# The feed-forward rows of the last two pairs turned by TensorE in halves, in a gated cross-attention block

## The chip, the cores and the metric

The kernel runs on one core of one Trainium2 chip. The metric is the device time of one execution in microseconds (us); of several executions the median counts. The engines are called by their names in the profile: PE (TensorE, with PEld for its weight loads), DVE (VectorE), ACT (ScalarE), POOL (GpSimd) and SP (SyncE, which here only issues DMAs).

## What is computed

A block of Flamingo's kind: 16 batches of 224 tokens of 512 channels attend to up to 750 context rows each, and then pass a feed-forward layer whose two products are quantised ("bitlinear": the rows to 8-bit whole numbers, the weights to -1, 0, 1). The reference, cut to what matters:

```python
def bitlinear(x, w, b):
    xq = act_quant(rmsnorm(x))      # row / rms, then round(row * 127 / max|row|)
    wq = weight_quant(w)            # -1, 0, 1, times a scale
    return einsum('bsd,fd->bsf', xq, wq) + b

def ffn(x):                         # 512 -> 2048 -> 512
    h = bitlinear(x, w1, b1)
    h = gelu(h, approximate=False)
    return bitlinear(h, w2, b2)

x = x + tanh(g_xattn) * attention(layernorm(x), ctx, mask, W_q, W_k, W_v, W_o, b_o)
x = x + tanh(g_ffn) * ffn(layernorm(x))
```

## The kernel before

The masked context rows are left out before the attention, and the batches are sorted by how many rows remain; the token rows follow in that order. The feed-forward doesn't care for batches: it works on the 3584 token rows as 28 tiles of 128 rows, two tiles to a pair, 14 pairs (0 to 13). While batch `s` is in its attention, the feed-forward pieces of earlier pairs are merged between the attention's pieces by their estimated costs. After the last batch there are still pair 12's up product and pair 13's whole way to do. This tail is written out by hand at the end of `compact_path`, and nothing else runs beside it. A scheduler fixes each engine's order when the kernel is built, by the order of the calls and by its own cost estimates, so the program that runs has one fixed list of instructions per engine, and semaphores between them.

The stages of one tile (`k` is 0 or 1, `i` the pair), with their lines:

- `project` and `normalise`: the attention's output product (PE L1214), the residual `y` (DVE L1217), the normalised and rounded row `xq`, which a DMA transpose on SP turns into `xqT` (L1262). On POOL, small steps give the row's factor `c1`, and `b2` is added to `y` (L1272).
- `up(i, k, g)`, g = 0, 1: eight fp8 products of 512 columns into a PSUM tile `hp` (PE L1284), then `h = hp * c1 + b1` for 1024 columns on DVE (L1292). `hp` has two buffers. `h`, 2048 columns in fp32, has two buffers, so that pair 13's tile 0 takes the memory of pair 12's tile 0.
- `gelu(i, (k,))`: Gelu on ACT in place (L1304), the row's largest magnitude on DVE (L1307), its inverse (L1225, L1226), the product rounded into int16 (`hq`, L1310), a cast of that to bf16 (L1311), and a DMA transpose on SP, `hqT<-hq` (L1313). Then ACT squares `h` in place and sums the squares (L1315), and POOL makes of the sum, in five small steps (L1317, L794, L1233 to L1235), the factor `c2`.
- `down(i, k)`: sixteen fp8 products of 512 columns with `hqT` as weights into the PSUM tile `fp` (PE L1329), `y = fp * c2 + y` on DVE (L1333), and the row write to memory, an indirect DMA that POOL issues (L1335).

`fp`, like the turned tiles of other stages, is taken from a PSUM pool of four buffers (`gen`). The tail interleaves these stages so:

```python
for k in range(2):
    project(i, k)
    normalise(i, (k,))                                  # i = 13
downs = down_pieces(i - 1) + down_pieces(i)
for _, piece in up_pieces(i - 1):                       # pair 12
    piece()
for _, piece in weave(up_pieces(i), downs[:2]) + downs[2:]:
    piece()
```

The memory that the change takes for itself: `pT` holds the turned attention weights of one batch (12 x 224 floats per partition) and `xoT` the attention's output of the last four batches (4 x 896 floats); both are read for the last time before the tail's up products.

Of the kernel before, what the change touches and what calls it, by code (L numbers as in the profile page):

```python
# [16 lines left out]
EPS = 1e-5  # L17
# [716 lines left out]
def compact_path(ctx, tc, sh, x, context, out, late_loads, stages):  # L734
# [3 lines left out]
    nc = tc.nc  # L738
    P = 128
    B, S, D = x.shape  # L740
    _, J, C = context.shape
    FF = sh.FF
# [4 lines left out]
    ND = D // P  # L747
    NC = C // P
    NF = FF // P
    NP = HEADS // 2  # L750
    NB = 512
# [445 lines left out]
    pairs = {}  # L1197
    late = {}
# [24 lines left out]
    def quantiser(amax, part, least, name):  # L1223
        k = small(f"k_{name}")
        nc.vector.tensor_scalar(k[:, part], amax[:, part], least, 1.0 / 127.0, ALU.max, ALU.mult)  # L1225
        nc.vector.reciprocal(k[:, part], k[:, part])  # L1226
        load["v"] += 300
        return k

    def unquantiser(amax, r, part, isw, name):  # L1230

        c = small(f"c_{name}")
        nc.gpsimd.tensor_tensor(c[:, part], amax[:, part], r[:, part], ALU.mult)  # L1233
        nc.gpsimd.tensor_scalar(c[:, part], c[:, part], 1e-5, None, ALU.max)
        nc.gpsimd.tensor_scalar(c[:, part], c[:, part], isw, None, ALU.mult)  # L1235
        return c
# [38 lines left out]
    def up(i, k, g):  # L1275
        f = pairs[i]
        if g == 0:
            f["h", k] = pa.tile([P, FF], F32, tag="h", name=f"h_{i}_{k}", bufs=2)
        h = f["h", k]
        ph = wide([P, 2, NB], F32, f"hp_{i}_{k}_{g}")  # L1280
        for n in range(2):
            at = (2 * g + n) * NB
            for d in range(ND):
                nc.tensor.matmul(  # L1284
                    ph[:, n, :],
                    lhsT=f["xqT"][:, k * ND + d, :],
                    rhs=w1T[:, d, at : at + NB],
                    start=(d == 0),
                    stop=(d == ND - 1),
                )  # L1290
        cols = slice(2 * g * NB, 2 * (g + 1) * NB)
        nc.vector.scalar_tensor_tensor(  # L1292
            h[:, cols], ph.rearrange("t i n -> t (i n)"), f["c1", k], sh.b1[:, cols], ALU.mult, ALU.add
        )
        load["v"] += 1280

    def gelu(i, ks=(0, 1)):
        f = pairs[i]
        name = f"{i}_{ks[0]}"
        part = slice(ks[0], ks[-1] + 1)  # L1300
        ss = small(f"ss_{name}")
        amax = small(f"a2_{name}")
        for k in ks:
            nc.scalar.activation(f["h", k], f["h", k], AF.Gelu)  # L1304
        for k in ks:
            h = f["h", k]
            nc.vector.tensor_reduce(amax[:, k : k + 1], h, AX.X, ALU.max, apply_absolute_value=True)  # L1307
            scale = quantiser(amax, slice(k, k + 1), 1e-5 * EPS**0.5, f"2_{i}_{k}")
            hq = late["rows"].tile([P, FF], BF16, tag="hq", name=f"hq_{i}_{k}", bufs=3)
            nc.vector.tensor_scalar(hq.bitcast(I16), h, scale[:, k : k + 1], None, ALU.mult)  # L1310
            nc.vector.tensor_copy(hq, hq.bitcast(I16))  # L1311
            f["hqT", k] = hqT = late["rows"].tile([P, NF, P], BF16, tag="hqT", name=f"hqT_{i}_{k}", bufs=2)
            nc.sync.dma_start_transpose(out=hqT, in_=hq)  # L1313
        for k in ks:
            nc.scalar.activation(f["h", k], f["h", k], AF.Square, accum_out=ss[:, k : k + 1])  # L1315
# [6 lines left out]
        load["v"] += len(ks) * (2282 + 1280 + 690)  # L1322
        load["s"] += len(ks) * 2 * 1910 + 2600

    def down(i, k):
        f = pairs[i]
        po = gen([P, D], F32, f"fp_{i}_{k}")
        for n in range(NF):
            nc.tensor.matmul(  # L1329
                po, lhsT=f["hqT", k][:, n, :], rhs=w2T[:, n, :], start=(n == 0), stop=(n == NF - 1)  # L1330
            )
        y = f["y"][:, k, :]
        nc.vector.scalar_tensor_tensor(y, po, f["c2", k], y, ALU.mult, ALU.add)  # L1333
        load["v"] += 700
        nc.gpsimd.indirect_dma_start(  # L1335
            out=out_rows,
            out_offset=bass.IndirectOffsetOnAxis(ap=token(2 * i + k), axis=0),
            in_=y,
            in_offset=None,
            bounds_check=B * S - 1,  # L1340
            oob_is_err=False,
        )

    NPAIR = NTOK // 2

    def up_pieces(i):
        p = []
        for k in range(2):
            p += [(1.8, lambda g=g, k=k: up(i, k, g)) for g in range(2)]
            p.append((0.0, lambda k=k: gelu(i, (k,))))  # L1350
        return p

    def down_pieces(i):
        return [(3.5, lambda k=k: down(i, k)) for k in range(2)]

    def project_pieces(i):
        p = [(1.8, lambda k=k: project(i, k)) for k in range(2)]
# [134 lines left out]
    _, normed_first = norm_first(0)  # L1492
# [5 lines left out]
    pa = ctx.enter_context(tc.tile_pool(name="pa", bufs=1))  # L1498
# [39 lines left out]
    for s in range(B):  # L1538
# [35 lines left out]
    i = NPAIR - 1  # L1574
    residual(i)
    for k in range(2):
        project(i, k)
        normalise(i, (k,))
    downs = down_pieces(i - 1) + down_pieces(i)
    for _, piece in up_pieces(i - 1):  # L1580
        piece()
    for _, piece in weave(up_pieces(i), downs[:2]) + downs[2:]:
        piece()

# [31 lines left out]
```

## Time and profile before

| | |
|---|---|
| median of 3 runs | 751.12 us |
| lowest, highest | 750.07, 753.04 us |
| the profiled execution | 751.76 us |
| span in the profile | 750.0 us |
| mean granted PE clock | 0.976 |
| last row write issued by POOL | 737.75 us from the start of the span |

Busy time over the span, from the page: PE 681.3 us (91%), PEld 434.5 (58%), DVE 499.0 (67%), ACT 408.0 (54%), POOL 394.1 (53%). The tail from 697 on is 53 us, 7% of the span, and has its own limits, which the shares of the whole don't tell.

How the views are read. A row of the timeline has the start, the length, the engine, the line of the kernel, the operation, what it writes and reads with the shapes, and the count of instructions merged; in brackets stands how long the engine had been idle and what it waited for. A row of the windows has for each engine the busy time and the count of instructions in that stretch, then the granted clock of PE as a share of full speed, the DMA engines' busy share and the GB/s moved. A row by form has the busy time in all, the mean ns of one instruction, and the idle time before. The matmuls' ends are modelled; the times of POOL are rough.

### The profile page before, as it was taken

The numbers are of one execution on the slowest core, as the hardware profiler recorded it, in microseconds if no ns is written. First come the engines' busy times: TensorE is split into PE (matmuls) and PEld (weight loads), VectorE is DVE, ScalarE is ACT, GpSimd is POOL, SyncE is SP. The second block draws the span as 40 slices with busy tenths as digits, with TensorE's granted clock in tenths as the row PEclk, the third lists the DMA queues.
The fourth block names the chain that finished last, engine by engine and source line by source line (L and its number), as shares of the span: only waits on it lengthen the run. The fifth ranks groups of instructions, "written<-read, shape, count | busy, mean of one in ns | idle before, by whom it ended". The sixth has DMA issues, their size and how long they took to land.

```text
span 750.0 us, 11362 instructions
## 1 busy us (share of the span) xinstructions
PE 681.3 (91%) x3900; PEld 434.5 (58%) x3900; DVE 499.0 (67%) x1284; ACT 408.0 (54%) x963; POOL 394.1 (53%) x541
## 2 busy tenths in 40 slices
PE   4998899999999999997999999999999999988652
PEld 3776677675656565665655665666666566443211
DVE  5586846876684684755758675588584939586860
ACT  2549645383673846635757368365565656460530
POOL 5583676463654644547366564565654453636141
PEclk9989999999999999999999999999999999999887
DMA  7794031022222312222142413123132222214250
GB/s 240 270 285 140 25 90 31 15 73 57 76 48 62 95 43 74 50 66 73 28 99 68 85 54 68 43 72 79 55 62 65 56 71 57 71 29 78 41 108 31
DMA packets 87218, 58.77 MB, mean 78 GB/s; under 512 B 75488, under 2 KB 75632, under 8 KB 87024
## 3 DMA queue, kind: packets, MB, share of 16 engines
q1 hardware_dynamic: 79024, 32.00, 18.6%
q0 software_dynamic: 8128, 25.96, 11.0%
q8 instruction: 33, 0.54, 0.3%
q14 instruction: 33, 0.27, 0.1%
HBM read 32.26 MB, written 7.34 MB: 53 GB/s over the span
## 4 chain that ended last, share of the span: by engine, by line
PE 55%; issue 13%; DVE 12%; POOL 11%; DMA 4%; ACT 3%; POOLq 0%; DVEq 0%; ACTq 0%; SPq 0%
PE qp L1035 9%; PE op L1214 9%; PE fp L1329 7%; PE hp L1284 6%; PE kp L916 5%; PE sim L1074 4%; PE vp L931 4%; POOL p L1108 2%; PE ptp L1128 2%; DVE a L1307 2%; PE av L1151 2%; DVE h L1292 2%; DMA hqT<-hq 2%; DVE hq L1310 1%; POOL y L1272 1%
## 5 line engine op out<-in xcount | busy, mean ns | idle before, releaser
L1108 POOL TENSOR_TENSOR p<-p,rec 112x768 f32<-112x768 f32 (+1 forms) x64 | 84.3, 1318 | 73.6 <-DVE rec L1107 28.5
L1329 PE MATMUL fp<-w2T,hqT 128*128 128x512 fp8e4 x448 | 104.5, 388 | 13.6 <-DMA hqT<-hq 13.6
L1284 PE MATMUL hp<-w1T,xqT 128*128 128x512 fp8e4 x448 | 107.1, 384 | 8.8 <-DVE h L1292 6.1
L1098 ACT ACTIVATE p<-p,nm 112x192 f32<-112x192 f32 (+1 forms) x256 | 106.5, 420 | 8.0 <-DVE nm L1088 7.8
L1035 PE MATMUL qp<-xnT,wq_sb 128*128 128x224 f32 x512 | 105.8, 361 | 0.6 <-ACT xnT L780 0.6
L1214 PE MATMUL op<-wo_sb,xoT 128*128 128x512 f32 x224 | 103.7, 599 | 0.0
L1035 PEld LDWEIGHTS qp<-xnT,wq_sb 128*128 128x128 f32 x512 | 97.5, 194 | 6.6 <-issue 3.3
L1292 DVE SCALAR_TENSOR_TENSOR h<-hp,c,b_bc 128x1024 f32<-128x1024 f32 x56 | 71.6, 1279 | 40.1 <-PE hp L1284 37.6
L1329 PEld LDWEIGHTS <-hqT 128*128 128x128 bf16 x448 | 43.3, 99 | 71.1 <-DMA hqT<-hq 16.7
L1088 DVE CUSTOM_DVE_ANT_0 p<-sim,mask 112x128 f32<-112x128 f32 (+1 forms) x224 | 57.9, 313 | 34.4 <-PE sim L1074 33.9
L1307 DVE TENSOR_REDUCE a<-h 128x1 f32<-128x2048 f32 x28 | 63.9, 2281 | 22.4 <-ACT h L1304 22.3
L1284 PEld LDWEIGHTS <-xqT 128*128 128x128 bf16 x448 | 43.2, 98 | 57.7 <-issue 15.4
L1333 DVE SCALAR_TENSOR_TENSOR y<-fp,c,y 128x512 f32<-128x512 f32 x28 | 20.9, 745 | 76.2 <-PE fp L1329 72.9
L1335 POOL DMA_INDIRECT out_dram<-y,token x28 | 30.9, 1104 | 75.9 <-DVE y L1333 70.4
L1315 ACT ACTIVATE h<-h 128x2048 f32<-128x2048 f32 x28 | 53.4, 1907 | 22.2 <-DVE hq L1310 14.8
L1304 ACT ACTIVATE h<-h 128x2048 f32<-128x2048 f32 x28 | 53.4, 1909 | 19.7 <-DVE k L1225 10.8
L916 PE MATMUL kp<-ctxT,wk_sb 128*128 128x192 f32 (+1 forms) x384 | 63.3, 314 | 0.0
L1214 PEld LDWEIGHTS op<-wo_sb,xoT 128*128 128x128 f32 x224 | 40.7, 190 | 38.8 <-issue 36.3
L916 PEld LDWEIGHTS kp<-ctxT,wk_sb 128*128 128x128 f32 x384 | 57.6, 198 | 6.2 <-issue 4.3
L1272 POOL TENSOR_TENSOR y<-y,b_bc 128x512 f32<-128x512 f32 x28 | 36.6, 1309 | 37.6 <-DVE fx L1253 37.4
L780 ACT COPY pT<-ptp 128x448 f32<-128x448 f32 x62 | 32.3, 536 | 42.6 <-PE ptp L1128 40.4
L1074 PE MATMUL sim<-kT,qT 64*112 64x192 f32 (+1 forms) x512 | 51.0, 313 | 1.7 <-issue 0.6
(173 smaller groups left out, 1172.4 us busy)
## 6 DMA issues: line engine op xcount, KB each, us to landing
raw<-in_L_ffn_w_dram SPq DMA_DIRECT2D x16, 512.0 KB
wq_sb<-in_L_xattn_W_q_dram SPq DMA_DIRECT2D x1, 1024.0 KB
b_bc<-in_L_ffn_b_dram SPq DMA_DIRECT2D x1, 1024.0 KB
wk_sb<-in_L_xattn_W_k_dram SPq DMA_DIRECT2D x1, 768.0 KB
wv_sb<-in_L_xattn_W_v_dram SPq DMA_DIRECT2D x1, 768.0 KB
wo_sb<-in_L_xattn_W_o_dram SPq DMA_DIRECT2D x1, 512.0 KB
wo_sb<-in_L_xattn_W_o_dram SPq DMA_DIRECT2D x2, 256.0 KB
y<-in_x_dram,token POOLq DMA_INDIRECT x28
```

Source lines behind the costliest of these rows:

```text
L916: nc.tensor.matmul(pk[:, p - p0, :], lhsT=sh.wk[:, c, p * P : (p + 1) * P], rhs=st["ctxT"][:, c, :cap], start=(c == 0), stop=(c == NC - 1),)
L1035: nc.tensor.matmul(pq[:, i, :], lhsT=sh.wq[:, d, (p + i) * P : (p + i + 1) * P], rhs=st["xnT"][:, d, :], start=(d == 0), stop=(d == ND - 1),)
L1074: nc.tensor.matmul(sim[:, j, i, :cap], lhsT=st["qT"][j * DH : (j + 1) * DH, p, q * TQ : (q + 1) * TQ], rhs=st["kT"][j * DH : (j + 1) * DH, ...
L1088: nc.vector.tensor_tensor_reduce(out=probs[:, h, :cap], in0=sim[:, j, i, :cap], in1=st["mask"][:, j * begin : j * begin + cap], scale=-(DH ...
L1098: nc.scalar.activation(probs[:, h, :cap], probs[:, h, :cap], AF.Exp, bias=nmax, scale=-1.0, accum_out=total[:TQ, h : h + 1],)
L1108: nc.gpsimd.tensor_tensor(probs[:, :, :cap], probs[:, :, :cap], rec[:TQ].unsqueeze(2).to_broadcast([TQ, 4, cap]), ALU.mult,)
L1214: nc.tensor.matmul(po, lhsT=xoT[:, d, at : at + P], rhs=sh.wo[:, d, :], start=(d == 0), stop=(d == ND - 1))
L1284: nc.tensor.matmul(ph[:, n, :], lhsT=f["xqT"][:, k * ND + d, :], rhs=w1T[:, d, at : at + NB], start=(d == 0), stop=(d == ND - 1),)
L1292: nc.vector.scalar_tensor_tensor(h[:, cols], ph.rearrange("t i n -> t (i n)"), f["c1", k], sh.b1[:, cols], ALU.mult, ALU.add)
L1304: nc.scalar.activation(f["h", k], f["h", k], AF.Gelu)
L1307: nc.vector.tensor_reduce(amax[:, k : k + 1], h, AX.X, ALU.max, apply_absolute_value=True)
L1329: nc.tensor.matmul(po, lhsT=f["hqT", k][:, n, :], rhs=w2T[:, n, :], start=(n == 0), stop=(n == NF - 1))
```

## The change

All pairs up to 11 stay as they are. For pairs 12 and 13 the DMA transposes of `hq` are replaced: PE turns each 128 x 128 block against an identity matrix, eight blocks into one PSUM tile of `gen`, and ACT copies that tile into half of `hqT`. The core of the diff:

```diff
+    def turn_by_tensor(i, k):
+        for g in range(2):
+            pt = gen([P, NF // 2, P], BF16, f"hqp_{i}_{k}_{g}")
+            for n in range(NF // 2):
+                at = g * FF // 2 + n * P
+                nc.tensor.transpose(pt[:, n, :], hq[:, at : at + P], ident16)
+            turned = nc.scalar.copy(hqT[:, g * NF // 2 : (g + 1) * NF // 2, :], pt)
+        return turned.ins
...
     def gelu(i, ks=(0, 1)):
...
-            nc.vector.tensor_copy(hq, hq.bitcast(I16))
-            nc.sync.dma_start_transpose(out=hqT, in_=hq)
+            if i < NPAIR - 2:
+                nc.vector.tensor_copy(hq, hq.bitcast(I16))
+                nc.sync.dma_start_transpose(out=hqT, in_=hq)
+                continue
+            for g in range(2):
+                cols = slice(g * half, (g + 1) * half)
+                nc.scalar.copy(hq[:, cols], hq.bitcast(I16)[:, cols])
```

So pair 12 has its casts on ACT, in halves; its squares and its `c2` move into a function `measure`, called where the tail wants it. Pair 13 has functions of its own:

```diff
+    def up_last(i, k):
+        if k == 0:
+            place = pa.tile([P, 12, S], F32, tag="pT", name="h_last", bufs=1)
+            h = place.rearrange("p n q -> p (n q)")[:, :FF]
+        else:
+            h = xoT.rearrange("p n q -> p (n q)")[:, :FF]
+        for g in range(2):
...
+            nc.vector.scalar_tensor_tensor(
+                h[:, cols], ph.rearrange("t i n -> t (i n)"), f["c1", k], sh.b1[:, cols], ALU.mult, ALU.add
+            )
+            nc.scalar.activation(h[:, cols], h[:, cols], AF.Gelu)
+            nc.vector.tensor_reduce(most[:, g : g + 1], h[:, cols], AX.X, ALU.max, apply_absolute_value=True)
+    def gelu_last(i, k):
+        nc.vector.tensor_reduce(amax[:, part], f["most", k], AX.X, ALU.max)
+        scale = quantiser(amax, part, 1e-5 * EPS**0.5, f"2_{name}")
+        for g in range(2):
+            nc.vector.tensor_scalar(hq.bitcast(I16)[:, cols], h[:, cols], scale[:, part], None, ALU.mult)
+            rounded = nc.vector.tensor_copy(hq[:, cols], hq.bitcast(I16)[:, cols])
+    def measure_last(i, k):
+        for g in range(2):
+            nc.scalar.activation(junk, f["h", k][:, 2 * g * NB : 2 * (g + 1) * NB], AF.Square,
+                                 accum_out=squares[:, g : g + 1])
+        nc.gpsimd.tensor_tensor(r[:, part], squares[:, 0:1], squares[:, 1:2], ALU.add)
...
+    def down(i, k, between=None):
...
+            if between and n == NF // 2 - 1:
+                with tc.issue_after(last.ins):
+                    f["turned"] = turn_by_tensor(*between)
```

(`junk` is written to buffers of the tag `x` rather than over `h`.) `down` leaves out the `y` step and the row write, which are now `store(i, k)`. The tail becomes:

```diff
+    for k in range(2):
+        for _, piece in ups[3 * k : 3 * k + 3]:
+            piece()
+    for k in range(2):
+        up_last(i, k)
+    measure(i - 1, (0,))
+    turn_by_tensor(i - 1, 0)
+    down(i - 1, 0, (i - 1, 1))
+    down(i - 1, 1)
+    with tc.issue_after(pairs[i - 1]["turned"]):
+        measure(i - 1, (1,))
+    rounded = [gelu_last(i, k) for k in range(2)]
+    for k in range(2):
+        with tc.issue_after(rounded[k]):
+            store(i - 1, k)
+    with tc.issue_after(pairs[i - 1]["turned"]):
+        measure_last(i, 0)
+    turn_by_tensor(i, 0)
+    down(i, 0, (i, 1))
+    store(i, 0)
+    with tc.issue_after(pairs[i]["turned"]):
+        measure_last(i, 1)
+    down(i, 1)
+    store(i, 1)
```

`tc.issue_after(x)` asks the scheduler to place what is inside after the instruction `x` in the order, without a wait of its own. In the built program each engine's order up to VectorE's last `h` step of pair 12 (L1292, at 696.38 us before) is the same as before. From there, ACT has: the Gelus of pair 12 and of pair 13's first tile, the casts of pair 12's tile 0 (two), its two turned copies, the casts of tile 1, the Gelus of pair 13's tile 1 in halves, the square of pair 12's tile 0, the two turned copies of tile 1, its square, the two half squares of pair 13's tile 0, the four turned copies of pair 13, and its last two half squares. POOL has the `c2` of pair 12's two tiles and of pair 13's first, three row writes, the last `c2`, and the last row write.

More of the change, by code (lines that the diff above doesn't have):

```diff
@@ L1295, in up @@
         load["v"] += 1280
+    def turn_by_tensor(i, k):
+        f = pairs[i]
+        hq, hqT = f["hq", k], f["hqT", k]
+        for g in range(2):
[5 more added lines that the diff above has]
+        return turned.ins
     def gelu(i, ks=(0, 1)):
@@ L1310, in gelu, with measure @@
             nc.vector.tensor_scalar(hq.bitcast(I16), h, scale[:, k : k + 1], None, ALU.mult)
-            nc.vector.tensor_copy(hq, hq.bitcast(I16))
             f["hqT", k] = hqT = late["rows"].tile([P, NF, P], BF16, tag="hqT", name=f"hqT_{i}_{k}", bufs=2)
-            nc.sync.dma_start_transpose(out=hqT, in_=hq)
+            if i < NPAIR - 2:
+                nc.vector.tensor_copy(hq, hq.bitcast(I16))
+                nc.sync.dma_start_transpose(out=hqT, in_=hq)
+                continue
+            half = FF // 2
+            for g in range(2):
+                cols = slice(g * half, (g + 1) * half)
+                nc.scalar.copy(hq[:, cols], hq.bitcast(I16)[:, cols])
+            f["hq", k] = hq
+        f["ss", ks], f["a2", ks] = ss, amax
+        if i < NPAIR - 2:
+            measure(i, ks)
+        load["v"] += len(ks) * (2282 + 1280 + 690)
+        load["s"] += len(ks) * 2 * 1910 + 2600
+    def measure(i, ks):
+        f = pairs[i]
+        name = f"{i}_{ks[0]}"
+        part = slice(ks[0], ks[-1] + 1)
+        ss, amax = f["ss", ks], f["a2", ks]
         for k in ks:
@@ L1321, in gelu @@
             f["c2", k] = c[:, k : k + 1]
-        load["v"] += len(ks) * (2282 + 1280 + 690)
-        load["s"] += len(ks) * 2 * 1910 + 2600
-    def down(i, k):
+    def up_last(i, k):
+        f = pairs[i]
+        if k == 0:
[3 more added lines that the diff above has]
+            h = xoT.rearrange("p n q -> p (n q)")[:, :FF]
+        most = small(f"am_{i}_{k}")
+        for g in range(2):
+            ph = wide([P, 2, NB], F32, f"hp_{i}_{k}_{g}")
+            for n in range(2):
+                at = (2 * g + n) * NB
+                for d in range(ND):
+                    nc.tensor.matmul(
+                        ph[:, n, :],
+                        lhsT=f["xqT"][:, k * ND + d, :],
+                        rhs=w1T[:, d, at : at + NB],
+                        start=(d == 0),
+                        stop=(d == ND - 1),
+                    )
+            cols = slice(2 * g * NB, 2 * (g + 1) * NB)
+            nc.vector.scalar_tensor_tensor(
+                h[:, cols], ph.rearrange("t i n -> t (i n)"), f["c1", k], sh.b1[:, cols], ALU.mult, ALU.add
+            )
+            nc.scalar.activation(h[:, cols], h[:, cols], AF.Gelu)
+            nc.vector.tensor_reduce(most[:, g : g + 1], h[:, cols], AX.X, ALU.max, apply_absolute_value=True)
+        f["h", k], f["most", k] = h, most
@@ new lines, in gelu_last @@
+    def gelu_last(i, k):
+        f = pairs[i]
+        name = f"{i}_{k}"
+        part = slice(k, k + 1)
+        h = f["h", k]
+        amax = small(f"a2_{name}")
+        nc.vector.tensor_reduce(amax[:, part], f["most", k], AX.X, ALU.max)
+        scale = quantiser(amax, part, 1e-5 * EPS**0.5, f"2_{name}")
+        hq = late["rows"].tile([P, FF], BF16, tag="hq", name=f"hq_{name}", bufs=3)
+        f["hqT", k] = hqT = late["rows"].tile([P, NF, P], BF16, tag="hqT", name=f"hqT_{name}", bufs=2)
+        half = FF // 2
+        for g in range(2):
+            cols = slice(g * half, (g + 1) * half)
+            nc.vector.tensor_scalar(hq.bitcast(I16)[:, cols], h[:, cols], scale[:, part], None, ALU.mult)
+            rounded = nc.vector.tensor_copy(hq[:, cols], hq.bitcast(I16)[:, cols])
+        f["hq", k], f["a2", k] = hq, amax
+        return rounded.ins
@@ new lines, in measure_last @@
+    def measure_last(i, k):
+        f = pairs[i]
+        name = f"{i}_{k}"
+        part = slice(k, k + 1)
+        squares = small(f"sq_{name}")
+        for g in range(2):
+            junk = pa.tile([P, 2, D], F32, tag="x", name=f"sq_{name}_{g}", bufs=3)
+            nc.scalar.activation(
+                junk.rearrange("p k d -> p (k d)"),
+                f["h", k][:, 2 * g * NB : 2 * (g + 1) * NB],
+                AF.Square,
+                accum_out=squares[:, g : g + 1],
+            )
+        r = small(f"r2_{name}")
+        nc.gpsimd.tensor_tensor(r[:, part], squares[:, 0:1], squares[:, 1:2], ALU.add)
+        nc.gpsimd.tensor_scalar(r[:, part], r[:, part], 1.0 / FF, EPS, ALU.mult, ALU.add)
+        pow_half(r[:, part])
+        c = unquantiser(f["a2", k], r, part, sh.isw[1], f"2_{name}")
+        f["c2", k] = c[:, part]
@@ L1328, in down, with store @@
         for n in range(NF):
-            nc.tensor.matmul(
+            last = nc.tensor.matmul(
                 po, lhsT=f["hqT", k][:, n, :], rhs=w2T[:, n, :], start=(n == 0), stop=(n == NF - 1)
             )
+            if between and n == NF // 2 - 1:
+                with tc.issue_after(last.ins):
+                    f["turned"] = turn_by_tensor(*between)
+        f["po", k] = po
+    def store(i, k):
+        f = pairs[i]
+        po = f["po", k]
         y = f["y"][:, k, :]
@@ L1353, in down_pieces, with both @@
     def down_pieces(i):
-        return [(3.5, lambda k=k: down(i, k)) for k in range(2)]
+        def both(k):
+            down(i, k)
+            store(i, k)
+        return [(3.5, lambda k=k: both(k)) for k in range(2)]
     def project_pieces(i):
@@ L1578, in compact_path @@
         normalise(i, (k,))
[L1579 to L1583, printed above, removed]
+    ups = up_pieces(i - 1)
+    for k in range(2):
[22 more added lines that the diff above has]
+    store(i, 1)
 _INS = [
```

## The prediction

> **What bounds the kernel now.** I read the kernel's share of busy time first (PE 91% over the whole span), and leave it aside: the change touches only what follows the last attention batch, from about 697 us on. There I read the timeline, then the waits, then the windows with the granted clock. Times are us from the span's start. The timeline of PE alone, 700 to 740:
>
> ```profile
> 705.13 1.01 PE L1284 MATMUL hp<-w1T,xqT 128*128 128x512 fp8e4 x2 [5.43 <-DVE h L1292]
> 706.73 5.41 PE L1329 MATMUL fp<-w2T,hqT 128*128 128x512 fp8e4 x16 [0.59 <-DMA hqT<-hq]
> 711.97 3.19 PE L1284 MATMUL hp<-w1T,xqT 128*128 128x512 fp8e4 x14
> 715.13 3.63 PE L1329 MATMUL fp<-w2T,hqT 128*128 128x512 fp8e4 x16
> 727.95 8.50 PE L1329 MATMUL fp<-w2T,hqT 128*128 128x512 fp8e4 x32 [9.19 <-DMA hqT<-hq]
> ```
>
> PE, busy in the average, works here in bursts. Its last burst, the down products of pair 13, starts 9.19 us after the one before, when a DMA transpose has landed. The same stretch among the waits (engine, line, waited for: total, times, longest):
>
> ```profile
> PEld L1329 <- DMA hqT<-hq: 11.6, 3, 9.7
> PE fp L1329 <- DMA hqT<-hq: 9.8, 2, 9.2
> DVE h L1292 <- ACT h L1315: 1.5, 1, 1.5
> ```
>
> The third line is VectorE waiting for the `h` buffer that ScalarE is still squaring. The windows (busy time and count by engine, then granted clock, DMA share, GB/s):
>
> ```profile
> 703.50:710.40 6.90, 4.68 (x11) 1.45 (x11) 6.51 (x7) 2.05 (x4) 1.48 (x5) 0.51 0.40 76
> 717.20:720.60 3.40, 1.56 (x8) 0.49 (x5) 3.33 (x6) 2.30 (x2) 0.00 (x0) 1.00 0.00 0
> 720.60:724.00 3.40, 0.00 (x0) 0.00 (x0) 3.30 (x5) 1.50 (x2) 2.74 (x6) 1.00 0.52 91
> 724.00:730.90 6.90, 2.95 (x8) 1.05 (x9) 1.66 (x2) 2.00 (x2) 2.53 (x6) 0.51 0.76 151
> ```
>
> VectorE is busy 6.51 of 6.90 and 3.33 of 3.40: until 725.7, when its last cast ends, it sets the pace and the transposes hang off it. After that nobody works but the DMA and PE. And PE's clock falls to half after each long idle stretch: the 16 matmuls at 706.73 take 5.41 us, those at 715.13 take 3.63. The end, from the timeline:
>
> ```profile
> 736.55 0.75 DVE L1333 SCALAR_TENSOR_TENSOR y<-fp,c,y 128x512 f32<-128x512 f32 x1 [2.70 <-PE fp L1329]
> 737.75 0.98 POOL L1335 DMA_INDIRECT out_dram<-y,token  x1 [2.51 <-DVE y L1333]
> ```
>
> The last row write is issued at 737.75; the span ends at 750.0, and these 12.3 us I hold fixed. The chain of the page puts the end on POOL's small steps of c; the timeline shows that y waits for fp, so I follow the timeline.
>
> **What the Trainium skill says.** "TensorE: Matmul & The Clock Gate", Part 1, says PE drops to half rate after about one idle window of 3.4 us and recovers after about one busy one. The trace agrees: half rate begins at 703.5 and 724, after 3.8 and 5.1 us without a matmul, and lasts some 6.9. It also shows what the page leaves open: a window with 1.56 of 3.40 us busy (717.2) is not punished. "SBUF — State Buffer", Who interferes with whom, says two-port VectorE instructions and GpSimd lock each other out; the c step of POOL that runs beside the hq product at 723.67 takes 1.34 us in place of 0.30. As a price I use "ScalarE: Activation LUTs", What ACT_TABLE_LOAD costs: 186 ns + 0.833 ns per element, back-to-back overlapped by some 93 ns. The trace: 1.91 us for 2048 elements (1.89 by the page), and a square at 672.46 of 1.91 us whose accumulator read starts at 674.27, 0.10 early.
>
> **The change, part by part.** Rows by form give most prices (busy, mean ns):
>
> ```profile
> L1392 ACT ACTIVATE junk<-raw 128x1024 f32<-128x1024 f32 x10 | 10.7, 1070 | 0.1
> L780 ACT CAST w2T<-wp 128x1024 fp8e4<-128x1024 bf16 x7 | 7.2, 1023 | 2.2 <-PE wp L1437 2.2
> L1388 DVE TENSOR_REDUCE wsums<-raw 128x1 f32<-128x1024 f32 x6 | 7.1, 1204 | 0.0
> L1261 DVE CAST xq<-xq 128x1024 bf16<-128x1024 int16 x13 | 5.6, 432 | 0.4
> ```
>
> *Removed:* four DMA transposes on SP. The first lands 4.28 us after its issue at 702.40. The third follows a cast that ends at 721.05 and frees PE only at 727.95, 6.9 us later, since it shares the DMA engines with a row write (issued 720.74) and the fourth transpose. Nothing is queued behind them on SP. *Added on PE:* 8 transposes per half; the weight stage does 8 such in 0.61 us (97.59) at full rate and in 1.04 us at half rate (45.22). *Added on ScalarE:* eight copies out of PSUM at 1.02 us, four casts of pair 12. No row shows an int16-to-bf16 cast there: from 0.95 us (an overlapped 1024-wide activation) to 1.25 (VectorE's PSUM cast is 1.22); I take 1.04, by the page's formula. Gelu by halves: 1.06 each, from 1.91 less 1024 x 0.833 ns. Squares by halves: 1.07 plus a 0.19 read. So ScalarE, with about 16 us to do in the tail before, gets about 30: it becomes the bound. *VectorE:* loses two casts of 0.69; pair 13 in halves costs 2 x 1.20 for 2.28 on the reduction, 2 x 0.75 for 1.29 on the product (interpolated between 0.49 at 512 and 1.29 at 2048), 2 x 0.43 for 0.69, and one small reduction of 0.16. *Own memory for pair 13's h* ends the 1.5 us wait. *Moved:* up products of pair 13 ahead of all down products; the stores of pair 12 behind the rounding of pair 13; on POOL three row writes (1.10 us each) ahead of the last c.
>
> Now the sum, with the engines' orders as the built program has them. VectorE from 697.61: two reductions (4.56), two h steps of pair 13 slipped in (2.56), the first hq product (1.29): done at 706.05; small steps hide in the overlaps. ScalarE then never waits: from 706.13, by start-to-start steps, 4 casts x 0.95, 4 copies of pair 12 x 0.93, 2 gelu halves x 0.97, 2 squares with reads x 1.92, 2 half squares with reads x 1.07 = 3.80 + 3.72 + 1.94 + 3.84 + 2.14 = 15.44. The copy of pair 13's first turned half, which is queued behind all of these, starts at 721.57 and ends at 722.59. (Its input is ready earlier: rounding ends at 718.04, PE has done pair 12 at 720.25 and the two turns at 721.2.) PE: 8 matmuls, two turns and 8 matmuls, 4.44 us, to 727.11. VectorE's y, 0.07 + 0.75, to 727.93. POOL issues that row after 0.40 (737.30 to 737.75 in the trace: 0.45) for 1.10, to 729.43. Only then, in POOL's order, come the six steps of the last c: 0.20 + 0.19 + 0.57 + 0.19 + 0.23 + 0.30 and gaps, to 731.21 (the last squares end at 729.05, the last matmul at 730.46: both hidden, by 0.4 and 0.8 us). Last y to 732.03, last issue at 732.43. Against 737.75: -5.3.
>
> Two additions. Pair 12's down product of tile 1 waits for a copy behind the square, so PE stands idle from 713.7 to 716.75. That is 3.05 us: depending on where the 3.41 us windows fall, one ends mostly idle and the next runs at half rate. Up to 1.7 us of extra PE time then eat the 1.4 us of slack before 722.67, and delay pair 13 by up to 0.93; trying fourteen positions of the windows in the same schedule gave 0 to 0.93, 0.6 in the mean. Further, each second half square writes the tile that the first wrote, so it cannot overlap: 0.1. The new wait of VectorE's y of pair 12 on the late c holds pair 13's second rounding back by under 0.6 us through POOL's lockout; 3 us of ScalarE work hide it. I take -4.6.
>
> The profiled execution took 751.76, 1.76 more than its span; less 4.6 it is 747.2. The median of the three runs is 0.64 lower, 751.12, so the forecast is 746.5.
>
> **Rivals.** *Less comes of it:* ScalarE's instructions alternate between buffers and PSUM banks with semaphores between; if none overlaps, the same schedule moves the end to 734.2 (-3.55), and the half-rate window takes another 0.9: -2.65, 748.5. For it: the whole path is ScalarE's; against it: reads, copies and squares of different tiles overlap all over the trace. *More comes of it:* the window falls well and casts and copies take 0.95: -5.7, 745.4. *Slower:* PE keeps half rate from 714 to the end. Then 16 matmuls take 6.8 us and 8 turns 1.04; the schedule ends at 742.45, +4.7, 755.8. It decides once half rate holds for more than two windows on the path after 722. Against it: at half rate PE would be busy almost without a break, and every such window of the trace (707 to 710.4) ended the half rate. *It doesn't do what it says:* excluded as to the transposes, as the built program's SP has none after pair 13's xqT.
>
> **Numbers.** The forecast -4.6 with its neighbours (-3.9 to -5.3) has 0.58, more 0.12, less 0.24, slower 0.06. A measurement tells about 0.5% here, 3.8 us; so faster 0.70, same 0.24, slower 0.06. The range runs from 744.4 (more, and the 1 us by which runs lie below the median) to 749.6 (less, and as much above); it leaves out the slow case and the tails.
>
> **What would show it.** Counted from the table load of gelu at 694.4: the first cast on ScalarE some 11.7 us later, ScalarE unbroken for 15 us, the copies of pair 13 at 27 to 28, its first down product done at 33 to 34, the last row write issued at 38.0 to 39 (43.4 before). Wrong if ScalarE shows gaps, if its casts take over 1.25, if the last c ends before the third row write, or if the clock is at half for more than one window.

## The result, and the profile after

| | before | after |
|---|---|---|
| median of 14 runs each | 752.28 us | 750.71 us |
| lowest, highest | 749.70, 756.68 us | 748.48, 754.63 us |
| the profiled execution, its span | 751.76, 750.0 us | 748.97, 747.2 us |
| gelu's table load, the tail's start | 694.38 us | 693.02 us |
| from there to the last row write's issue | 43.37 us | 41.88 us |

The ratio is 0.9984, with a 95% interval of 0.9965 to 1.0003: no change that this measurement can tell, where -4.6 us was forecast. Single runs of one kernel differ by up to 7 us, mostly with the granted PE clock (0.967 to 0.980 in the runs of after), so I use the last row of the table as the yardstick: it holds nothing but the changed tail. It comes from one execution of each kernel, so PE's clock can move it too, by 1.8 us in one case below (e1b). Times with a plus count from the table load. The profiled execution is 2.8 us shorter, but 1.36 of that was there before the tail began, where nothing is changed; the tail gained 1.49.

The timeline of after, in the lines that answer to those shown of before:

```profile
714.93 5.31 PE L1424 MATMUL fp<-w2T,hqT 128*128 128x512 fp8e4 x16 [2.98 <-ACT hqT L1305]
720.78 1.93 ACT L1305 COPY hqT<-hqp 128x1024 bf16<-128x1024 bf16 x2 [1.02 <-PE hqp L1304]
722.92 1.12 POOL L1438 DMA_INDIRECT out_dram<-y,token  x1 [0.48 <-issue]
726.48 0.75 DVE L1436 SCALAR_TENSOR_TENSOR y<-fp,c,y 128x512 f32<-128x512 f32 x1 [5.32 <-PE fp L1424]
726.55 0.97 POOL L1438 DMA_INDIRECT out_dram<-y,token  x1 [2.52 <-DMA out_dram<-y,token]
730.71 0.97 POOL L1438 DMA_INDIRECT out_dram<-y,token  x1 [3.19 <-DMA out_dram<-y,token]
734.90 1.10 POOL L1438 DMA_INDIRECT out_dram<-y,token  x1 [1.07 <-DVE y L1436]
```

The DMA transposes are gone, and PE's 9 us hole with them. Pair 13's first sum `y` ends at 727.23. But the row write of that sum, the third of four, is issued at 730.71, and the bracket says for what POOL waited: the landing (all its data written, its semaphore set) of a DMA of the same name, the row write before it. The waits of the same stretch (total, times, longest) and the chain that ended last (start, us, what) say the same:

```profile
DVE y L1436 <- POOL c L1235: 8.1, 3, 6.6
POOL out_dram L1438 <- DMA out_dram<-y,token: 5.7, 2, 3.2
```

```profile
722.92 2.87 DMA out_dram<-y,token
...
726.55 3.39 DMA out_dram<-y,token
729.99 0.73 issue
730.71 0.97 POOL out_dram L1438
```

A row write lands 2.87 or 3.39 us after its issue, and 0.76 us later the next one is issued. All row writes go to one tensor, `out`, at rows that only the token list knows; in the built program each carries a wait for the semaphore of the one before it. The first line of the waits follows from it: its longest, 6.6 us, is the last sum's wait for its `c`, which stands behind the third row write in POOL's queue.

This wait was there before the change, and I passed over it. The end of the chain of before:

```profile
734.14 2.84 DMA out_dram<-y,token
736.98 0.02 issue
...
737.75 0.98 POOL out_dram L1335
```

There the last sum ended at 737.30, and from a sum's end to the issue 0.45 us pass; from the landing at 736.98 to the issue it is 0.77. Either way leads to 737.75: the two waits ended together.

### The profile page after: what moved, and what is told of

It reads as the page before. It is cut to its first block, busy times and chain, and to the rows that moved or that the text cites. A ratio compares the mean times of both kernels' runs of the same rounds, so it can differ in the third digit from the quotient of the medians.

```text
span 747.2 us, 11515 instructions
## 1 busy us (share of the span) xinstructions
PE 682.8 (91%) x3964; PEld 436.8 (58%) x3964; DVE 497.6 (67%) x1290; ACT 420.0 (56%) x981; POOL 396.4 (53%) x543
## 3 DMA queue, kind: packets, MB, share of 16 engines
q1 hardware_dynamic: 70704, 29.90, 17.5%
## 4 chain that ended last, share of the span: by engine, by line
PE 52%; DVE 13%; issue 12%; POOL 10%; ACT 6%; DMA 4%; POOLq 0%; ACTq 0%; DVEq 0%
PE qp L1035 9%; PE op L1214 8%; PE fp L1424 7%; PE hp L1284 6%; PE kp L916 4%; PE sim L1074 4%; PE vp L931 4%; PE ptp L1128 2%; PE av L1151 2%; POOL p L1108 2%; DVE a L1318 2%; DMA out_dram<-y,token 2%; DVE h L1292 2%; DVE hq L1321 1%; DVE p L1088 1%
## 5 line engine op out<-in xcount | busy, mean ns | idle before, releaser
L1284 PE MATMUL hp<-w1T,xqT 128*128 128x512 fp8e4 x416 | 99.8, 384 | 3.4 <-DVE nm L1088 1.9
L1292 DVE SCALAR_TENSOR_TENSOR h<-hp,c,b_bc 128x1024 f32<-128x1024 f32 x52 | 66.5, 1280 | 38.3 <-PE hp L1284 38.0
L1318 DVE TENSOR_REDUCE a<-h 128x1 f32<-128x2048 f32 x26 | 59.3, 2282 | 22.4 <-ACT h L1315 22.3
L1284 PEld LDWEIGHTS <-xqT 128*128 128x128 bf16 x416 | 40.3, 98 | 48.6 <-issue 10.2
L1344 ACT ACTIVATE h<-h 128x2048 f32<-128x2048 f32 x26 | 49.7, 1910 | 17.1 <-DVE hq L1321 9.6
L1315 ACT ACTIVATE h<-h 128x2048 f32<-128x2048 f32 x26 | 49.6, 1909 | 9.0 <-DVE h L1292 8.8
```

The costliest lines, as they stand in the source:

```text
L1284: nc.tensor.matmul(ph[:, n, :], lhsT=f["xqT"][:, k * ND + d, :], rhs=w1T[:, d, at : at + NB], start=(d == 0), stop=(d == ND - 1),)
L1292: nc.vector.scalar_tensor_tensor(h[:, cols], ph.rearrange("t i n -> t (i n)"), f["c1", k], sh.b1[:, cols], ALU.mult, ALU.add)
```

## The experiments

Tile 13.0 is tile 0 of pair 13. Theory 1: the gain is lost to the chain of the four last row writes, each of which waits for the landing of the one before, and to POOL's order, which starts this chain late (the first row's sum was there at 717.90, but two more `c` stood ahead of its write) and puts the last `c` behind the third write. Rivals: PE's half-rate stretch (5.31 us for 16 products in place of 3.63) took it; POOL's small steps, slowed by VectorE, took it; ScalarE's path is worth less than priced.

After has the 14 runs from above; the others have 6 to 22 runs each, against the kernel before. "First" to "last" are the issues of the four row writes; "sum" is the start of pair 13's first `y`. The kernels named "aside" write two or three of the last four tiles to tensors of their own, so these rows are missing from the output.

| kernel | first | second | third | last | sum | median, us | ratio (95%) |
|---|---|---|---|---|---|---|---|
| before | 18.90 | 26.36 | 39.76 | 43.37 | 38.72 | 751.5 to 752.6 | 1 |
| after | 29.90 | 33.53 | 37.69 | 41.88 | 33.46 | 750.71 | 0.9984 (0.9965 to 1.0003) |
| e1 aside | 29.82 | 31.24 | 34.48 | 38.68 | 33.46 | 747.56 | 0.9934 (0.9914 to 0.9954) |
| e1b before, aside | 18.88 | 26.34 | 41.58 | 45.20 | 40.54 | 751.64 | 0.9990 (0.9979 to 1.0002) |
| e2 POOL's order | 25.15 | 29.55 | 33.88 | 38.23 | 32.84 | 747.81 | 0.9945 (0.9925 to 0.9964) |
| e6 one square moved | 30.52 | 34.16 | 37.66 | 41.87 | 32.32 | 751.38 | 0.9985 (0.9970 to 1.0000) |
| e10 casts back | 31.00 | 34.96 | 38.53 | 42.74 | 32.29 | 753.43 | 1.0016 (0.9999 to 1.0032) |
| e4 = e2, squares later | 25.82 | 30.22 | 35.20 | 39.55 | 33.51 | 748.94 | 0.9951 (0.9930 to 0.9972) |
| e5 = e4, c on VectorE | 25.82 | 30.25 | 35.20 | 38.77 | 32.63 | 746.86 | 0.9929 (0.9909 to 0.9949) |
| e11 = e5, aside | 25.83 | 30.25 | 33.67 | 37.09 | 32.63 | 745.66 | 0.9913 (0.9888 to 0.9939) |
| e8 = e2, squares early | 24.01 | 28.79 | 34.89 | 39.23 | 32.09 | 747.53 | 0.9935 (0.9913 to 0.9957) |
| e12 = e8, c on VectorE | 24.01 | 29.45 | 33.98 | 37.47 | 29.81 | 747.05 | 0.9938 (0.9919 to 0.9958) |
| e13 = e12, aside | 24.00 | 29.44 | 30.83 | 34.50 | 29.80 | 744.45 | 0.9909 (0.9879 to 0.9940) |

### Without the wait (e1_aside, e1b_before_aside)

```diff
+        rows = out_rows
+        if i == NPAIR - 2:
+            rows = nc.dram_tensor(f"aside_{k}", (B * S, D), F32, kind="Internal").ap()
         nc.gpsimd.indirect_dma_start(
-            out=out_rows,
+            out=rows,
```

> The changed kernel, with pair 12's two row writes sent to two DRAM tensors of their own instead of the output (so the output lacks pair 12's rows); nothing else differs. The yardstick is the time from gelu's table load to the issue of the last row write: 43.4 us before, 41.9 us with the change, 38.8 us if the forecast had held.
> Theory 1 (the gain is lost because each row write waits for the landing of the one before it): the second row write follows the first by its own 1.1 us, the third (pair 13, tile 0) is issued 0.4 to 0.5 us after its sum y at about +34.2, the last at 38.6 to 39.0, about 3.1 us less than the changed kernel. Against the kernel before: -4.6 us, a ratio near 0.994.
> Rivals (TensorE's half-rate stretch and its idle gaps; POOL's steps slowed by VectorE; ScalarE's path worth less than priced): nothing of these is touched, so 41.9 stays and the ratio is that of the changed kernel, 0.998.

The timeline of POOL in this kernel:

```profile
726.95 1.12 POOL L1441 DMA_INDIRECT aside<-y,token  x1 [0.41 <-issue]
728.37 0.98 POOL L1441 DMA_INDIRECT aside<-y,token  x1 [0.30 <-issue]
731.61 0.97 POOL L1441 DMA_INDIRECT out_dram<-y,token  x1 [2.26 <-DVE y L1436]
735.81 1.10 POOL L1441 DMA_INDIRECT out_dram<-y,token  x1 [1.07 <-DVE y L1436]
```

With the table load at 697.13, the last issue is at +38.68: 3.2 us less than after, with the same orders on all engines. The third write now waits for its sum, nothing else, and PE's half-rate stretch is as in after (16 products in 5.31 us). The ratio, too, lies apart from that of after (up to 0.9954; after from 0.9965). This settles it for theory 1; the rivals expected 41.9. As for POOL's small steps, slowed by VectorE: in after they delay the start of the chain a little. The squares of tile 13.0 were read by 719.76, and their first POOL step began at 720.33, so this costs the first row write 0.6 us at most.

The same edit on the kernel before:

> The same edit on the kernel before: pair 12's two row writes go to DRAM tensors of their own, the output lacks those rows. Theory 1: before the change the last sum y came as late as the landing of the third row write, so taking the wait away gains next to nothing: 43.4 us from table load to last row write (43.0 to 43.5), ratio 1.000. If instead the wait for a landing was a cost of its own before too, this falls below 42.5. The rivals expect 43.4.

The ratio, 0.9990, is as expected: no gain. The yardstick is not: 45.20. In the profiled execution PE's 32 last products took longer,

```profile
727.21 10.03 PE L1329 MATMUL fp<-w2T,hqT 128*128 128x512 fp8e4 x32 [9.47 <-DMA hqT<-hq]
```

10.03 us in place of 8.50: a longer half-rate stretch after the idle hole (the granted clock is still 0.76 in the mean from 729.9 to 736.8; in before it is 1.00 from 730.9 to 734.3). The last write followed its sum by 0.46 us, as before. This run says less than its expectation claims. Its edit frees the third row write, which did not wait for a landing in before; the last one still had to wait for the third, which landed 2.85 us after its issue, in time for the sum. So that the two waits tied in before is read from its trace, and not tested.

### POOL's order alone (e2_early)

```diff
+    with tc.issue_after(rounded[0]):
+        written = store(i - 1, 0).ins           # pair 12, tile 0
+    with tc.issue_after(written):
+        measure(i - 1, (1,), (1,))              # its next tile's c
+    with tc.issue_after(rounded[1]):
+        written = store(i - 1, 1).ins
+    with tc.issue_after(written):
+        measure_last(i, 0, (1,))                # pair 13's first c
```

(The last argument splits `measure`: 0 are the squares on ScalarE, 1 the steps of `c`. The same order is given to the last `c`; these lines are left out.)

> The changed kernel with POOL's queue in another order at the end and nothing left out: each row write of pair 12 stands right behind the factor c of its own tile, ahead of the c of the next tile. In the changed kernel the first of the four row writes was issued 5 us after its sum y was there, because two more c stood ahead of it.
> Theory 1 (chain of row writes, each waiting for the landing of the one before): the first write at +25 to 25.5 instead of +29.9, the second 3.6 to 4.7 behind it, the third when its y is there (+34.6), the last at 38.6 to 39.2: about 3 us less than the changed kernel, ratio to the kernel before near 0.994.
> Rivals (TensorE at half rate, or ScalarE's path): the changed kernel's 41.9 stays. POOL slowed by VectorE as the cause: the c of tile 13.0 comes later than before, so 41.9 or more.

It came so: first +25.15, last +38.23, ratio 0.9945. No write waits for a landing any more; what holds them 4.3 us apart is POOL's own round, of which the timeline of POOL shows one:

```profile
727.18 1.10 POOL L1445 DMA_INDIRECT out_dram<-y,token  x1 [1.07 <-DVE y L1443]
728.31 0.20 POOL L1421 TENSOR_TENSOR r<-sq 128x1 f32<-128x1 f32 x1
...
730.13 0.30 POOL L1235 TENSOR_SCALAR c<-c,isw 128x1 f32<-128x1 f32 x1
731.51 1.12 POOL L1445 DMA_INDIRECT out_dram<-y,token  x1 [1.07 <-DVE y L1443]
```

The issue takes 1.10, six steps of the next `c` 2.1, then the sum and the way to the next issue 1.07. Started 4.75 us earlier, the four writes are over 3.65 earlier. The landings are close behind: the second write landed 3.51 us after its issue, and with 0.76 to start again the third could have come 0.06 us before it did. So e2 has moved the start of the chain, and POOL's round and the landing now cost about the same.

### PE's half-rate stretch alone (e6_square_only)

```diff
-    measure(i - 1, (0,))
     turn_by_tensor(i - 1, 0)
     down(i - 1, 0, (i - 1, 1))
+    with tc.issue_after(pairs[i - 1]["turned"]):
+        measure(i - 1, (0,))
```

> The changed kernel with one step moved on ScalarE: the square of pair 12's tile 0 (1.9 us) stands behind the copies of tile 1's turned halves, not ahead of them. POOL's queue and the row writes keep their order. TensorE's idle gap of 3 us ahead of 16 down products goes, and with it the half-rate stretch of 5.3 us for these 16 (3.5 expected).
> Theory 1: the copies of pair 13's first turned half come up to 1 us earlier (+26.7 instead of +27.8), and that is worth nothing at the end: 41.7 to 41.9 us from table load to last row write, ratio that of the changed kernel.
> Rival (TensorE's half-rate stretch ate the gain): the last row write comes 1 us or more earlier, 40.9 or less.

From its timeline:

```profile
714.38 3.63 PE L1424 MATMUL fp<-w2T,hqT 128*128 128x512 fp8e4 x16 [1.09 <-ACT hqT L1305]
726.69 0.75 DVE L1436 SCALAR_TENSOR_TENSOR y<-fp,c,y 128x512 f32<-128x512 f32 x1 [3.57 <-PE fp L1424]
732.03 0.97 POOL L1438 DMA_INDIRECT out_dram<-y,token  x1 [2.53 <-DMA out_dram<-y,token]
736.24 1.10 POOL L1438 DMA_INDIRECT out_dram<-y,token  x1 [1.07 <-DVE y L1436]
```

The 16 products run at full rate (3.63), pair 13's first sum starts 1.14 us earlier than in after, and the last write is issued at +41.87 where it was +41.88. The half-rate stretch is real, but the gain is not lost there: the sum was there at 727.44, and its row write, held by a landing, was issued at 732.03. The equal end is in part chance. The moved square also made the first row write 0.62 us later (+30.52), and the landing of the second was 0.66 us quicker (2.73 in place of 3.39). Nor does the rate hang on this edit alone: e2 ran the 16 products in 3.63 us behind the same gap of 2.98 us that they have in after.

### One part undone (e10_casts_back)

```diff
-                nc.scalar.copy(hq[:, cols], hq.bitcast(I16)[:, cols])
+                nc.vector.tensor_copy(hq[:, cols], hq.bitcast(I16)[:, cols])
```

> The changed kernel with one part undone: pair 12's four half casts (1.05 us each) go back from ScalarE to VectorE (about 0.4 us each). ScalarE's unbroken stretch loses 4.2 us, VectorE's gets 1.5 us longer.
> Theory 1: what counts is when the chain of four row writes begins, and that waits for the c of tile 13.0, whose squares end ScalarE's stretch: these come about 2 us earlier, so the first row write is at +27.5 to 28.5 instead of +29.9, the last 12.0 us behind it, at 39.5 to 40.5 instead of 41.9.
> The forecast's own reading (ScalarE's stretch sets the end, then VectorE's): the copies of pair 13's first turned half about 2 us earlier, and the end as much. Rival (TensorE at half rate): no change, 41.9.

All three readings missed the number (42.74), and the miss speaks for the chain. Pair 13's copies came 1.15 us earlier and its first sum 1.17, yet the last write came 0.86 later, as the first one had (1.10). It did so because the squares of tile 13.0 ended no earlier (+26.7 in both kernels), and because one POOL step ran into VectorE's roundings:

```profile
721.90 2.02 POOL L1235 TENSOR_SCALAR c<-c,isw 128x1 f32<-128x1 f32 x1
```

2.02 us in place of 0.30. So here it is a POOL step, slowed by VectorE, that starts the chain later than in after. That the casts on ScalarE pay is seen on the yardstick alone (0.86 us): the intervals of the two ratios overlap.

### More of the path, same chain (e4_squares_last, e5_vector_c, e8_early_squares)

In e4, squares move behind turned copies, as in e6 and again for tile 13.0:

```diff
-    turn_by_tensor(i, 0)
+    turned = turn_by_tensor(i, 0)
+    with tc.issue_after(turned):
+        measure_last(i, 0, (0,))                # its squares
```

> The kernel with POOL's new order (row write of a tile right behind its own c), and with two squares moved on ScalarE as well: that of tile 12.0 behind the turned copies of 12.1, those of tile 13.0 behind the turned copies of 13.0. Copies of pair 13's first turned half then come 2 to 3 us earlier (+25 instead of +27.8), and TensorE has them earlier too.
> Theory 1, in the form it has now: after the reordering of POOL the end is set by POOL's own loop per tile (issue of a row write 1.1, the steps of the next c about 2.1, the sum y 0.75, 0.3 to the next issue: 4.3 us), which starts with the first row write; that one comes no earlier here (its square is even later). So 38.2 to 39.2 us from table load to last row write, no gain over the reordering alone (38.2).
> Rival (ScalarE's and TensorE's path to the first sum of pair 13 sets the end): 2 us less than the reordering alone, about 36.2.

In e5, on top of this, the `c` of the last three tiles is VectorE's work but for one step, and is no longer placed behind a row write (the part for tile 12.1):

```diff
-        nc.gpsimd.tensor_scalar(r[:, part], ss[:, part], 1.0 / FF, EPS, ALU.mult, ALU.add)
+        on = nc.vector if i == NPAIR - 2 and ks == (1,) else nc.gpsimd
+        on.tensor_scalar(r[:, part], ss[:, part], 1.0 / FF, EPS, ALU.mult, ALU.add)
         pow_half(r[:, part])
-        c = unquantiser(amax, r, part, sh.isw[1], f"2_{name}")
+        c = unquantiser(amax, r, part, sh.isw[1], f"2_{name}", on)
```

> As the kernel with two squares moved, and the factors c of tiles 12.1, 13.0 and 13.1 computed by VectorE but for their one power step, which stays on POOL. This takes about 1.5 us of POOL's 4.3 us loop per tile away, so that the wait for the landing of the row write before it is what is left.
> Theory 1: the four row writes are 3.6 to 4.2 us apart and no closer, whatever comes earlier on ScalarE, TensorE and VectorE; first at +25.6 to 26.2, last at 37.0 to 38.2.
> If the row writes did not wait for each other's landing, the last would come with its sum y at about 35.5.

In e8, pair 12's squares go by halves into ScalarE's idle time between the last gelus, and VectorE's rounding of tile 13.1 moves behind the first sum (of the edit, the new square):

```diff
+        return nc.scalar.activation(
+            junk, f["h", k][:, cols], AF.Square, accum_out=f["halves", k][:, g : g + 1]
+        ).ins
```

> POOL's new order, with pair 12's squares taken by halves: three of the four halves run in ScalarE's idle time of 1.5 and 2.4 us between the last gelus, one behind the turned copies of 12.1. Tile 12.0's factor c is then there before its product, and its row write, the first of the four, starts the chain earlier: its sum follows VectorE's rounding of tile 13.0.
> Theory 1: first row write at +23 to 24 instead of +25.2, each next one 4.3 us (POOL's loop) behind it, last at 36.0 to 37.2 us, 1 to 2 us less than the reordering alone; ratio to the kernel before near 0.992.
> Rival (the end is set by TensorE's clock): no gain over the reordering alone, 38.2 or more.

That these edits bring nothing, or little, over e2 was expected of e4 alone; the last write was later than I had said in all three (39.55, 38.77, 39.23), and in e5 the writes stood 4.43, 4.95 and 3.57 us apart, where 3.6 to 4.2 were expected. The chains show why: e5,

```profile
724.48 4.17 DMA out_dram<-y,token
729.43 2.79 DMA out_dram<-y,token
```

and e8:

```profile
724.16 5.32 DMA out_dram<-y,token
```

The second row write took 4.17 (4.19 in e4) and 5.32 us to land; I had reckoned with at most 3.4. The third was issued when that landing had come, though its sum had been there for 1.8 us in e5 and 2.0 in e8. e8's number is also what the rival expected (38.2 or more), but not for its reason: PE ran those 16 products in 3.63 us.

### With and without the chain once more (e11_vector_aside, e12_early_vector, e13_early_aside)

e12 has e8's early squares and e5's `c`; e11 and e13 are e5 and e12 with the first three of the four row writes aside:

```diff
+        if 2 * i + k in (24, 25, 26):
+            rows = nc.dram_tensor(f"aside_{i}_{k}", (B * S, D), F32, kind="Internal").ap()
```

> The kernel with c on VectorE and two squares moved (last row write at +38.8 us after gelu's table load), with the first three of the four last row writes sent to DRAM tensors of their own, so that none of the four waits for another (the output lacks those three tiles' rows).
> Theory 1: the third row write, which waited 3.3 us for the landing of the second, is issued with its sum y, at +33.6 instead of +35.2; the last c's power step stands behind it on POOL, so the last one comes about as much earlier, at 36.6 to 37.4. Rival (the landing is not what holds the writes apart): 38.8 stays.

> Both helps together, nothing left out: pair 12's squares early on ScalarE (first row write at +24.0), and the factors c of 12.1, 13.0 and 13.1 on VectorE but for the power step. Theory 1: four row writes 3.6 to 5 us apart, as each has to wait for the landing of the one before (landings took 2.8 to 5.3 us so far): first at +24.0, second at +28.4, the last at 36.4 to 38.5; ratio to the kernel before near 0.992. If the writes were free of each other, the last would be at about 35.

> The kernel with early squares and c on VectorE, with the first three of the four last row writes sent to DRAM tensors of their own (the output lacks those three tiles' rows). Theory 1: the third is issued with its sum at about +31.5, the last right behind its own sum, which waits for TensorE's last product (+33.2): 34.3 to 35.5, some 2 to 3 us less than with the chain of row writes; ratio near 0.989. Rival: no change from the kernel with the chain.

The last writes of all three came as expected: +37.09, +37.47, +34.50. The distances in e12 did not: 5.44, 4.53 and 3.49 us, where 3.6 to 5 were expected, and only the third write was held by a landing alone; the second waited for its sum, and for the last one the landing and the sum came together. The timelines of POOL of e12 and e13 side by side:

```profile
722.18 1.04 POOL L1462 DMA_INDIRECT out_dram<-y,token  x1 [1.15 <-DVE c L1234]
726.71 0.97 POOL L1462 DMA_INDIRECT out_dram<-y,token  x1 [3.50 <-DMA out_dram<-y,token]
730.20 1.04 POOL L1462 DMA_INDIRECT out_dram<-y,token  x1 [1.92 <-DVE y L1460]
```

```profile
723.49 1.04 POOL L1465 DMA_INDIRECT aside<-y,token  x1 [1.15 <-DVE c L1234]
724.88 0.97 POOL L1465 DMA_INDIRECT aside<-y,token  x1 [0.35 <-DVE y L1460]
728.55 1.04 POOL L1465 DMA_INDIRECT out_dram<-y,token  x1 [1.77 <-DVE y L1460]
```

The third write follows the second by 4.53 us with the chain and by 1.39 without. Of these 3.14 us the end keeps 2.97: +34.50 in place of +37.47. The medians differ by 2.6 us, but the intervals of the ratios overlap.

Of the kernels that write all of the output, e2, e4, e5, e8 and e12 beat the kernel before, by 0.49% to 0.71%; their intervals overlap, so these runs don't rank them. e2 is the smallest edit, and its interval (up to 0.9964) ends just under that of after (from 0.9965).

## Why the prediction was wrong, step by step

Times of after are put into the frame of before by adding 1.36.

- *VectorE until its first hq product, then ScalarE unbroken for 15.44 us from 706.13: right.* Measured: from 705.84 to 721.12, 15.28 us without a gap. The prices held; by form, ACT from 690 on (count, then total and mean ns):

```profile
L1305 ACT COPY hqT<-hqp 128x1024 bf16<-128x1024 bf16 x8 | 7.7, 1013 | 2.6 <-PE hqp L1304 2.6
L1330 ACT CAST hq<-hq 128x1024 bf16<-128x1024 int16 x4 | 4.0, 1049 | 0.1
```

  1.04 was taken for the cast that no row had shown, 1.02 for the copy.
- *The half-rate window delays pair 13 by 0 to 0.93: right, near the mean of 0.6.* The copies started at 722.14 (721.57 forecast, +0.57). ScalarE was done 0.45 early and then waited 1.02 us for PE. (One reading of the prediction is off: the idle stretch before 724 was 5.2 us, from 718.76, not 5.1.)
- *First down product of pair 13 at 727.11, its y at 727.93: right within the addition.* y ended at 728.59, +0.66; 0.7 had been added.
- *"POOL issues that row after 0.40 ... for 1.10, to 729.43": this step failed.* It took 3.48 us from the end of y to the issue (727.23 to 730.71 in after's own time), 3.0 more than the 0.45 of before. I had priced "three row writes (1.10 us each)" by what they occupy of POOL. Measured, they stand 3.63 and 4.16 us apart, since each waits for the landing of the one before: 2.87 to 3.39 us, and 0.76 to start again. And the first of them began late: by POOL's order, which I had read, two more `c` stood ahead of it, and I had asked only whether POOL's work would fit.
- *The last c behind the third write, the last y, the last issue: right in the sum.* 4.19 us from the third issue to the last; 4.10 forecast. Some luck is in it: the six steps of c took 2.13 with their gaps, where 1.78 was reckoned, and the issue (0.97 for 1.10) and the way from y to the issue (0.28 for 0.40) were shorter.

So of 3.1 us between forecast (-4.6) and tail (-1.5), 3.0 lie in one step, and e1, which takes the wait for the landing away from the second and the third write, gives back 3.2: its ratio, 0.9934, is a gain of 5.0 us (3.5 to 6.5), where 4.6 was forecast. The mechanism of the forecast, from the transposes to ScalarE's stretch, stood; what was late next was not asked at the output. Of the signs of being wrong that the prediction lists (gaps on ScalarE, slow casts, an early last c, a long half-rate stretch) none was seen: none of them asked when the first three row writes are issued.

Two places could have told me. The chain of waits of before put the landing of a row write into the last stretch, as shown above, and I set that view aside because the timeline named the sum. And "DMA: Bandwidth & Descriptors", in Anatomy of one DMA, gives a DMA issued from GpSimd about 2.0 us of fixed cost and 436 KB per us: for a row write of 262 KB an estimate of 2.6 us, against 2.84 in before; in Two DMAs through the same engine are not ordered, it says that a kernel has only the completion semaphore to order two DMAs by. The program waits for that semaphore, so row writes asked for closer than 3.6 us (2.84 and the 0.77 to start again) could have been expected to queue up; in before, the last two were 3.61 apart.

What stays open. Why the second row write's landing took 4.2 to 5.3 us in e4, e5 and e8 is not settled: the DMA view shows packets of the instruction queues in the same stretches, but also where landings were quick. Taking the wait alone away, with all writes going to the output, was not tried. In the kernel whose last write comes first, e12, the chain costs 3.0 us in the trace (e13).

## What to carry to other kernels

When a change brings the last results closer together, price the way out as a chain: how far apart successive writes to one tensor can be issued (landing plus restart where the program makes each wait for the one before, not the time that their issue takes), and when the first of them begins. A wait that ends at the same moment as the one you remove is the next bound. Here the chain that ended last named it where the timeline had another name in its brackets, so look at both. With engines that issue DMAs among other work, what stands ahead of a DMA in the queue is as much a part of the path as its data.

## What the runs showed of the hardware

- An indirect row write of 128 x 512 floats in the tail landed 2.71 to 3.78 us after its issue in most cases, 4.17 to 5.32 in three with no other row write in flight (e4, e5, e8). In the tail before, one that was issued at 720.74, beside DMA transposes, landed at 727.73.
- Small POOL steps beside VectorE roundings: a power step 1.24 us in place of 0.57 (after), a multiplication 2.02 in place of 0.30 (e10). "SBUF — State Buffer", Who interferes with whom, names this lock, as the prediction said; the price of one step was as long as VectorE's run beside it (721.76 to 723.83 in e10).
